# Constants behind the first graph's nodes, and the last two graphs' scaling re-divided between two engines

## The chip, the cores and the metric

The kernel runs on one core of a Trainium2 chip. The metric is the device time of one execution in microseconds (us), read as the median of several runs. A core has a matrix engine (TensorE, PE in the profile, with its weight loads listed apart as PEld), VectorE (DVE), ScalarE (ACT), GpSimd (POOL), and SyncE (SP), which in this kernel only issues transfers (DMA). Each engine works through its own queue of instructions in order, so an instruction that waits holds up all behind it on the same engine. Matrix products accumulate in PSUM, a small memory that TensorE writes and VectorE and ScalarE read; all other tiles lie in SBUF.

## The reference

Sixteen graphs (B = 16) of 1024 nodes with 256 features each pass two layers. `adj` is an integer matrix that holds only 0 and 1 here and is symmetric, so that of the four edge kinds of layer 0 only the one with weight vector `a0` occurs.

```python
# layer 0: gated aggregation
e0    = leaky(einsum('bid,bjd->bij', h * a0[:, 0], h))      # slope 0.2
alpha = sigmoid(where(adj == 1, e0, -max))                  # kinds 2 to 4 likewise with a1 to a3
x     = layernorm(x + einsum('bij,bjd->bid', alpha, h) + bias)

# layer 1: graph attention, 4 heads of 64 features
Wh    = (x @ W).reshape(B, N, 4, 64)
e     = leaky_relu(e_src[:, :, None] + e_dst[:, None, :])   # e_src = Wh.a_src, e_dst = Wh.a_dst per head
alpha = softmax(where(adj > 0, e, -1e9), axis=2)
x     = layernorm(x + elu(einsum('bijh,bjhf->bihf', alpha, Wh)))
```

## The kernel before

**Tiling.** Nodes go in 8 row blocks of 128 (index `jb` or `ib`), or in 2 halves of 512 columns, each half being two pairs of blocks. One graph is worked through in steps, and each step is a generator in `stages`; `issue` takes every step of every graph and issues them in the order of one number, `b * 112 + time`, where the times stand in three tables written into the kernel: `FIRST` for graph 0, `LAST` for graph 15 and `TIMES` for all others. Nothing reorders them afterwards, so these tables fix the order on every engine's queue. Steps of two to three neighbouring graphs are interleaved.

**Constants.** `load_constants` (L37 to L84) runs ahead of all graphs. On SP's queue it places the four columns `a_sb` (a0 to a3), the bias row, `w_aug` (the matrix W), then `a_src` broadcast to all partitions and `a_dst` in the same way. The two broadcast rows share one buffer, so `a_dst` (L63) waits until VectorE has multiplied W by `a_src`. VectorE forms the eight columns W·a_src and W·a_dst (four products of 128x256 and four sums), and the bias is split into a rounded high part and a rest (L75 to L83).

**Layer 0 of a graph.** `xload` (L237) brings the nodes `xb` (1 MB), `aload` (L243) brings one 512 KB block of the adjacency matrix at a time into one of two buffers `a32`, and `cast` (L252, ScalarE) turns it into bf16 in the single buffer `a16` and adds up its entries. `turn` transposes the block: graph 0 does so on TensorE, the other graphs by a DMA transpose. `mask` (L274, ScalarE) squares the transposed block into 8 bits, `mT`. Meanwhile the nodes are transposed (`xt`, `xtc`), scaled by a0 (`xta`), and multiplied (`score`); ScalarE and VectorE apply the leaky slope (`leak`, `leaky`), ScalarE the sigmoid. The scores are symmetric, so only the upper part is computed, and `lower` and `upper` (L379) multiply the mirrored and the direct part by the mask. `agg` (L390) aggregates over all blocks, and needs all eight masks. `residual`, `moments`, `spread` (GpSimd), `shift` and `norm` (L447, ScalarE) do the layer norm.

**Layer 1 of a graph.** `project` multiplies by `w_aug`, whose last eight columns give e_src and e_dst. `keep_rows` writes the e_src of each half as rows to DRAM (`sdram`), and `sload` reads the row of one head back, broadcast to 128 partitions (`sbc`). `exps` (L560 to L563) forms the exponentials `es` for both slopes s = 0 and 1, and `rho`. The exponential of a leaky sum is a product of a source and a target factor for each of the two slopes; so the kernel multiplies Wh by `es` (`product`, L576 on ScalarE for the last graph and L581 on VectorE for others), splits the result `gm` into a rounded high part (`high`, L594, ScalarE) and the rest (`low`, L601, VectorE), and multiplies by a matrix of zeros and ones, `pos` (L619, VectorE), that says at which edges the positive slope holds (`acc`, L631). The `gm` tile exists once, so the factors of the next graph come after the last product of this one that reads them. `acc` takes both PSUM buffers of its pool for one head in one half, and the next head begins when `acc_low` (L646, ScalarE) and `acc_sum` (L654, VectorE) have read both. `total` (L674) sums over all edges, which gives the negative slope by subtraction. `weigh` scales by `rho`, and `divide` takes the reciprocal `rzs` (L741) of the sum of the weights and scales by it; both scale through one helper, `times`: eight ScalarE instructions of one column factor each (L713) for the last graph, one VectorE instruction (L718) for the others. `elu`, `join`, and the second layer norm follow, and `leave` (L767) stores one half of 512 rows at a time.

**The end.** After the last graph, VectorE and TensorE reduce three checks (adjacency only 0 and 1, exponents in range, no overflow) to one `flag` (L1290), which the engines read; were it set, a slower general version would run. It is not set here.

Of the kernel before, what the change touches and what calls it, by code (L numbers as in the profile page):

```python
# [27 lines left out]
P = 128  # L28
HALF = 512
# [7 lines left out]
def load_constants(nc, const, work, x, a_list, bias, w, a_src, a_dst):  # L37
# [6 lines left out]
    k.F1 = F + 2  # L44
    k.ident = const.tile([P, P], F32, name="ident")
# [5 lines left out]

    k.a_sb = const.tile([P, k.DC, NK], F32, name="a_sb")
    for i, a in enumerate(a_list):
        nc.sync.dma_start(out=k.a_sb[:, :, i : i + 1], in_=a.rearrange("(c p) o -> p c o", p=P))
    bias_bc = work.tile([P, D], F32, tag="bias_bc", name="bias_bc")
    nc.sync.dma_start(out=bias_bc, in_=bias.partition_broadcast(P))


    k.w_aug = const.tile([P, k.DC, k.WD], F32, name="w_aug")
    nc.sync.dma_start(out=k.w_aug[:, :, 0:D], in_=w.rearrange("(c p) f -> p c f", p=P))  # L60
    for a, which in ((a_src, 0), (a_dst, 1)):
        a_bc = work.tile([P, D], F32, tag="a_bc", name=f"a_bc{which}")
        nc.sync.dma_start(out=a_bc, in_=a.rearrange("h f -> (h f)").partition_broadcast(P))  # L63
        for c in range(k.DC):
            prod = work.tile([P, D], F32, tag="prod", name=f"prod{which}_{c}")
            nc.vector.tensor_tensor(prod, k.w_aug[:, c, 0:D], a_bc, ALU.mult)
            dst = k.w_aug[:, c, D + which * H : D + which * H + H]
            nc.vector.tensor_reduce(dst, prod.rearrange("p (h f) -> p h f", h=H), AX.X, ALU.add)

# [5 lines left out]
    b_hi = work.tile([P, D], F32R, tag="b_hi", name="b_hi")  # L75
    nc.scalar.copy(b_hi, bias_bc)
    b_lo = work.tile([P, D], F32, tag="b_lo", name="b_lo")
    nc.vector.tensor_tensor(b_lo, bias_bc, b_hi.bitcast(F32), ALU.subtract)
    nc.vector.tensor_scalar(b_lo, b_lo, k.ident[:, 1:2], None, ALU.mult)
    k.bias_r = const.tile([P, D], F32R, name="bias_r")  # L80
    nc.vector.scalar_tensor_tensor(
        k.bias_r, b_hi.bitcast(F32), k.ident[:, 0:1], b_lo, ALU.mult, ALU.add
    )  # L83
    return k  # L84
# [105 lines left out]
class FastPools:  # L190
    def __init__(self, ctx, tc):
        def pool(name, bufs, **kw):
            return ctx.enter_context(tc.tile_pool(name=name, bufs=bufs, **kw))


        self.us = pool("f_us", 4)
        self.io = pool("f_io", 2)
        self.adjp = pool("f_adj", 2)
# [13 lines left out]
def stages(nc, k, pl, b, xg, adjg, outg, gm, sums, span, zinv):  # L212
# [9 lines left out]
    first, last = b == 0, b == k.B - 1  # L222
# [11 lines left out]

    def xload():
        t["xb"] = pl.io.tile([P, NB, D], F32, tag="xb", name="xb")
        nc.sync.dma_start(out=t["xb"], in_=xg.rearrange("(c p) d -> p c d", p=P))  # L237
        yield
# [186 lines left out]
    def spread(which):  # L425

        for half in range(NH):
            mvh = t["mv" + which][:, half * NQ : (half + 1) * NQ]
            v = small("std" + which, NQ)
            nc.gpsimd.tensor_scalar(v, mvh[:, :, 1], EPS, None, ALU.add)  # L430
            rstd = t["rstd" + which, half] = small("rstd" + which, NQ)
            nc.gpsimd.tensor_tensor(rstd, v, k.mhalf.to_broadcast([P, NQ]), ALU.pow)  # L432
            yield
# [9 lines left out]
    def norm(which):  # L443
        for ib in range(NB):
            half, q = divmod(ib, NQ)
            y = t["y", half][:, q, :]
            nc.scalar.activation(  # L447
                y, y, AF.Identity,
                bias=t["shift" + which, half][:, q : q + 1],
                scale=t["rstd" + which, half][:, q : q + 1],  # L450
            )
# [117 lines left out]
    def product():  # L569
        for h, s in FACTORS:  # L570
# [3 lines left out]
            if last:  # L574
# [16 lines left out]
    def high():  # L591
        for h, s in FACTORS:
            for cols, val in factor(h, s):
                nc.scalar.copy(gm[:, h, :, 0, s, cols], val)  # L594
# [746 lines left out]
```

## Time and profile before

| | us |
|---|---|
| runs, lowest to highest | 1781.34 to 1782.41 |
| runs, median of 3 | 1781.9 |
| the profiled execution's own time | 1781.79 |
| its span (first to last instruction) | 1780.0 |
| TensorE busy | 1718.5 |
| VectorE busy | 1624.8 |
| ScalarE busy | 1208.9 |
| GpSimd busy | 112.1 |

The page also cuts the span into 40 slices of 44.5 us and gives each engine's busy share in tenths:

```
PE   6999999999999999999999999999999999999883
DVE  4488999999999899999999999999999999999897
ACT  6583957759576684947759485784957668485665
PEclk9999999999999999999999999999999999999987
```

How to read it: a number after "L" is the line of the kernel; "out<-in" names the tiles that an instruction writes and reads; "xN" counts instructions; in square brackets stands the idle time of the engine ahead of the row, and the instruction whose end released it, as the profiler infers it. In a view in order of time, neighbouring instructions of one kind are put into one row with the start of the first. SPq is the queue of transfers that SP issues; a row there is the time of the issue, not of the transfer. The granted clock is the share of TensorE's full clock that the chip allowed.

### The profile page before, as it was taken

What the parts mean: (1) busy time and instruction counts of PE and PEld (TensorE: products, weight loads), DVE (VectorE), ACT (ScalarE), POOL (GpSimd) and SP (SyncE); (2) the same over time, 40 slices, a digit from 0 to 9 for tenths busy, and PEclk for the clock granted to TensorE, in tenths of its full rate; (3) what the DMA queues carried; (4) which work ended last, traced back from release to release, by engine and by line L of the source; (5) the groups of instructions that cost most, each with busy time, mean ns of one, the idle gap of its engine ahead of it and who ended that gap; (6) DMA issues with size and microseconds to landing.
All of it is one profiled execution on the core that took longest, in us unless ns stands there. A gap on an engine that the chain in (4) does not pass through costs nothing.

```text
span 1780.0 us, 29755 instructions
## 1 busy us (share of the span) xinstructions
PE 1718.5 (97%) x10707; PEld 1517.1 (85%) x10707; DVE 1624.8 (91%) x3581; ACT 1208.9 (68%) x2781; POOL 112.1 (6%) x138
## 2 busy tenths in 40 slices
PE   6999999999999999999999999999999999999883
PEld 4789898998979989898998979889898998989773
DVE  4488999999999899999999999999999999999897
ACT  6583957759576684947759485784957668485665
POOL 0000001010000101000010000101000010000100
PEclk9999999999999999999999999999999999999987
DMA  4452324524334343333424333353433425221020
GB/s 157 110 140 60 88 86 100 138 66 109 102 85 116 90 120 94 97 84 101 131 66 125 104 80 102 89 138 77 102 89 90 131 72 148 84 61 42 25 66 26
DMA packets 249243, 168.62 MB, mean 95 GB/s; under 512 B 133248, under 2 KB 232704, under 8 KB 249088
## 3 DMA queue, kind: packets, MB, share of 16 engines
q1 hardware_dynamic: 249088, 166.63, 35.0%
q8 instruction: 87, 1.43, 0.3%
q14 instruction: 68, 0.56, 0.1%
HBM read 118.10 MB, written 17.04 MB: 76 GB/s over the span
## 4 chain that ended last, share of the span: by engine, by line
PE 86%; issue 8%; ACT 2%; DVE 1%; POOL 1%; DMA 0%; POOLq 0%; ACTq 0%
PE acc L631 25%; PE agg L390 23%; PE tot L674 13%; PE e L323 13%; PE pw L479 6%; PE pg L362 3%; PE pt L287 1%; PE pt L460 1%; PE agg L386 1%; POOL rstd L432 1%; DVE pos L619 0%; ACT gm L594 0%; ACT a L252 0%; PE pbc L553 0%; ACT L349 0%
## 5 line engine op out<-in xcount | busy, mean ns | idle before, releaser
L619 DVE SCALAR_TENSOR_TENSOR pos<-sbc,nd,mT 128x512 fp32r<-128x512 f32 x1024 | 730.9, 743 | 35.6 <-PE acc L631 34.9
L631 PE MATMUL acc<-gm,pos 128*128 128x264 f32 x4096 | 629.0, 299 | 17.9 <-DVE rzs L741 6.0
L631 PEld LDWEIGHTS acc<-gm,pos 128*128 128x128 f32 x4096 | 547.7, 191 | 41.5 <-issue 15.9
L390 PE MATMUL agg<-xb,gate 128*128 128x256 f32 x2048 | 473.6, 379 | 0.0
L390 PEld LDWEIGHTS agg<-xb,gate 128*128 128x128 f32 x2048 | 374.0, 190 | 44.0 <-DVE gate L379 0.2
L674 PE MATMUL tot<-gm,allm 128*128 128x264 f32 x2048 | 321.3, 298 | 0.0
L674 PEld LDWEIGHTS tot<-gm,allm 128*128 128x128 f32 x2048 | 280.4, 189 | 4.0
L646 ACT COPY low<-acc 128x264 f32<-128x264 f32 x256 | 90.3, 378 | 279.9 <-PE acc L631 279.7
L323 PE MATMUL e<-xT,xTa 128*128 128x512 f32 (+3 forms) x768 | 269.2, 487 | 3.3 <-ACT xTa L311 1.6
L323 PEld LDWEIGHTS e<-xT,xTa 128*128 128x128 f32 x768 | 131.5, 190 | 92.8 <-issue 45.6
L666 ACT CAST allm<-mT 128x512 fp32r<-128x512 uint8 x256 | 157.0, 619 | 35.3 <-PE tot L674 34.9
L447 ACT ACTIVATE y<-y,shift,rstd 128x256 f32<-128x256 f32 x256 | 137.8, 592 | 45.1 <-DVE shift L440 45.0
L252 ACT ACTIVATE a<-a 128x1024 bf16<-128x1024 int32 x128 | 135.6, 1059 | 15.4 <-DMA aT<-a 7.9
L274 ACT ACTIVATE mT<-aT 128x1024 uint8<-128x1024 bf16 x120 | 127.1, 1059 | 16.0 <-DMA aT<-a 15.9
L430 POOL TENSOR_SCALAR std<-mv 128x4 f32<-128x4 f32 x64 | 30.1, 470 | 1653.1 <-DVE mv L413 1565.9
L479 PE MATMUL pw<-w_aug,yT 128*128 128x264 f32 x512 | 124.5, 386 | 0.5 <-ACT yT L469 0.5
L654 DVE TENSOR_TENSOR u<-acc,low 128x264 f32<-128x264 f32 x256 | 104.6, 420 | 12.8 <-ACT low L646 12.6
L343 DVE TENSOR_TENSOR gate<-e,gate 128x512 f32<-128x512 f32 x192 | 104.3, 551 | 9.2 <-ACT gate L335 8.8
L335 ACT ACTIVATE gate<-e 128x512 f32<-128x512 f32 x192 | 93.6, 488 | 18.4 <-PE e L323 18.3
L479 PEld LDWEIGHTS pw<-w_aug,yT 128*128 128x128 f32 x512 | 92.5, 190 | 13.8 <-ACT yT L469 1.3
L407 DVE BATCH_NORM_STATS2 st<-y 128x6 f32<-128x256 f32 x256 | 102.4, 415 | 0.6
L379 DVE TENSOR_TENSOR gate<-gate,mT 128x1024 f32<-128x1024 f32 (+7 forms) x128 | 95.0, 751 | 0.9 <-ACT mT L274 0.6
(101 smaller groups left out, 1817.2 us busy)
## 6 DMA issues: line engine op xcount, KB each, us to landing
a<-in_adj_dram SPq DMA_DIRECT2D x128, 512.0 KB, 4.9
sbc<-sdram SPq DMA_DIRECT2D x128, 256.0 KB, 4.5
xb<-in_x_dram SPq DMA_DIRECT2D x16, 1024.0 KB, 5.7
out_dram<-y SPq DMA_DIRECT2D x32, 512.0 KB, 3.5
aT<-a SPq DMA_TRANSPOSE x120, 3.1
sdram<-srow SPq DMA_DIRECT2D x32, 8.0 KB, 1.4
w_aug<-in_L_gnn_W_dram SPq DMA_DIRECT2D x1, 256.0 KB, 4.5
bias_bc<-in_L_gnn_bias_dram SPq DMA_DIRECT2D x1, 128.0 KB, 3.8
```

The costliest lines, as they stand in the source:

```text
L252: nc.scalar.activation(t["a16", ib], t["a32", ib], AF.Copy, accum_out=sums[:, 0, at : at + 1])
L274: nc.scalar.activation(t["mT"][:, :, ib * P : (ib + 1) * P], t["aT", ib], AF.Square, accum_out=sums[:, 1, at : at + 1],)
L323: nc.tensor.matmul(e[:, 0:n], lhsT=t["xTa", jb][:, c, :], rhs=t["xT"][:, c, at : at + n], start=(c == 0), stop=(c == DC - 1),)
L343: nc.vector.tensor_tensor(ge, t["e", jb, at][:, 0:n], ge, ALU.max)
L390: nc.tensor.matmul(agg[:, 0:D], lhsT=t["gate"][:, jb, ib * P : (ib + 1) * P], rhs=t["xb"][:, jb, :], start=False, stop=(jb == NB - 1),)
L447: nc.scalar.activation(y, y, AF.Identity, bias=t["shift" + which, half][:, q : q + 1], scale=t["rstd" + which, half][:, q : q + 1],)
L479: nc.tensor.matmul(pw[:, 0:WD], lhsT=t["yT"][:, c, jb * P : (jb + 1) * P], rhs=k.w_aug[:, c, :], start=(c == 0), stop=(c == DC - 1),)
L619: nc.vector.scalar_tensor_tensor(p_, t["sbc", half, h], t["nd"][:, jb, h : h + 1], t["mT"][:, jb, half * HALF : (half + 1) * HALF], ALU.is ...
L631: nc.tensor.matmul(t["acc", half, h, q // 2][:, q % 2, 0 : 4 * F1], lhsT=t["pos", half, h, jb][:, q * P : (q + 1) * P], rhs=gm[:, h, jb].r ...
L654: nc.vector.tensor_tensor(t["u", half, pair][:, :, h, :], t["acc", half, h, pair][:, :, 0 : 2 * F1], t["low", half, h, pair], ALU.add,)
L666: nc.scalar.copy(m_, t["mT"][:, j0 : j0 + 4, ib * P : (ib + 1) * P])
L674: nc.tensor.matmul(tot[:, 0 : H * F1], lhsT=t["allm", ib, jb // 4 * 4][:, jb % 4, :], rhs=gm[:, :, jb, l, 1, :], start=(jb == 0 and l == 0 ...
```

## The change

The change has five parts.

1. *Loading.* `load_constants` is divided into `shapes`, `make_constants` and a step `setup` of the first graph. `FastPools` opens the pools of nodes and adjacency first and the others later, in `fill`. Ahead of everything, graph 0's nodes are requested, in two halves, and its first two adjacency blocks; then `make_constants` requests only the column of `a0`. The five parts of `setup`, which do something in graph 0 only, are: request the two broadcast rows (each now with its own space) and W; form the eight weight columns; request the bias row and the other three columns; round the bias; form its rest. Their tiles come from the tag `sbc`, four buffers, which the products and the broadcast rows use later.
2. *Scaling.* In `times`, the ScalarE form holds for the last two graphs (14 and 15), where it held for the last one.
3. *Products.* In the last graph, ScalarE forms only the products of slope s = 1; those of s = 0 go to VectorE.
4. *Norm and store.* In the last graph's second half, the second norm of every other block goes to VectorE as one instruction of two scalars. The last half is stored in two parts.
5. *Order.* `FIRST` and `LAST` hold new times for all steps. `TIMES` is unchanged but for a row for `setup`, which does nothing there. `gm` is reached as `pl.gm`, and `rstd` is allocated ahead of `std`; neither alters an instruction.

```diff
-def load_constants(nc, const, work, x, a_list, bias, w, a_src, a_dst):
+def shapes(x, a_src):
     k = Consts()
...
+    return k
+
+def make_constants(nc, k, const, work):
...
-    for i, a in enumerate(a_list):
-        nc.sync.dma_start(out=k.a_sb[:, :, i : i + 1], in_=a.rearrange("(c p) o -> p c o", p=P))
-    bias_bc = work.tile([P, D], F32, tag="bias_bc", name="bias_bc")
-    nc.sync.dma_start(out=bias_bc, in_=bias.partition_broadcast(P))
...
+    a0 = k.inputs[0][0]
+    nc.sync.dma_start(out=k.a_sb[:, :, 0:1], in_=a0.rearrange("(c p) o -> p c o", p=P))
...
 class FastPools:
     def __init__(self, ctx, tc):
...
+        self.io = self.pool("f_io", 2)
+        self.adjp = self.pool("f_adj", 2)
+
+    def fill(self):
...
-    first, last = b == 0, b == k.B - 1
+    first, last, late = b == 0, b == k.B - 1, b >= k.B - 2
...
+    def two(name, dtype=F32):
+        tile = pl.work.tile([P, 2, D], dtype, tag="sbc", name=name, bufs=4)
+        return tile[:, 0], tile[:, 1]
+
+    def setup():
+        if not first:
+            yield from (None for _ in range(5))
+            return
+        a_list, bias, w, a_src, a_dst = k.inputs
+        rows = two("vecs")
+        for row, a in zip(rows, (a_src, a_dst)):
+            nc.sync.dma_start(out=row, in_=a.rearrange("h f -> (h f)").partition_broadcast(P))
+        nc.sync.dma_start(out=k.w_aug[:, :, 0:D], in_=w.rearrange("(c p) f -> p c f", p=P))
+        yield
+
+        for which in range(2):
+            for c, prod in enumerate(two("wa")):
+                nc.vector.tensor_tensor(prod, k.w_aug[:, c, 0:D], rows[which], ALU.mult)
+                dst = k.w_aug[:, c, D + which * H : D + which * H + H]
+                nc.vector.tensor_reduce(
+                    dst, prod.rearrange("p (h f) -> p h f", h=H), AX.X, ALU.add
+                )
+        yield
+
+        row, low = two("brow")
+        nc.sync.dma_start(out=row, in_=bias.partition_broadcast(P))
+        for i in range(1, NK):
+            nc.sync.dma_start(
+                out=k.a_sb[:, :, i : i + 1], in_=a_list[i].rearrange("(c p) o -> p c o", p=P)
+            )
+        yield
+        high, _ = two("bhigh", F32R)
+        nc.scalar.copy(high, row)
+        yield
+        nc.vector.tensor_tensor(low, row, high.bitcast(F32), ALU.subtract)
+        nc.vector.tensor_scalar(low, low, k.ident[:, 1:2], None, ALU.mult)
+        nc.vector.scalar_tensor_tensor(
+            k.bias_r, high.bitcast(F32), k.ident[:, 0:1], low, ALU.mult, ALU.add
+        )
+        yield
+
     def xload():
         t["xb"] = pl.io.tile([P, NB, D], F32, tag="xb", name="xb")
-        nc.sync.dma_start(out=t["xb"], in_=xg.rearrange("(c p) d -> p c d", p=P))
+        parts = NH if first else 1
+        for i in range(parts):
+            c = slice(i * NB // parts, (i + 1) * NB // parts)
+            nc.sync.dma_start(
+                out=t["xb"][:, c, :], in_=xg.rearrange("(c p) d -> p c d", p=P)[:, c, :]
+            )
         yield
...
+            if last and which == "1" and half and q % 2:
+                nc.vector.tensor_scalar(y, y, rstd, shift, ALU.mult, ALU.add)
+            else:
+                nc.scalar.activation(y, y, AF.Identity, bias=shift, scale=rstd)
...
-            if last:
+            if last and s:
                 for jb in range(NB):
                     nc.scalar.activation(
                         prod[:, jb, :], t["wh"][:, jb, h * F : (h + 1) * F], AF.Copy,
...
     def times(val, by):
-        if last:
+        if late:
...
         for half in range(NH):
-            nc.sync.dma_start(
-                out=outg[half * HALF : (half + 1) * HALF].rearrange("(c p) d -> p c d", p=P),
-                in_=t["y", half],
-            )
+            parts = 2 if last and half else 1
+            rows = outg[half * HALF : (half + 1) * HALF].rearrange("(c p) d -> p c d", p=P)
+            for i in range(parts):
+                c = slice(i * NQ // parts, (i + 1) * NQ // parts)
+                nc.sync.dma_start(out=rows[:, c, :], in_=t["y", half][:, c, :])
...
 FIRST = {
-    "xload": [-2609.24],
-    "aload": [-1820.92, -1748.01, -1728.96, -1693.97, -1643.68, -1598.12, -1550.35, -1517.97],
+    "aload": [-144.60, -143.90, -143.00, -141.40, -140.70, -140.00],
+    "cast": [-144.70, -144.30, -143.50, -142.40, -141.10, -140.60, -139.50, -138.20],
+    "setup": [-143.30, -141.90, -141.00, -139.70, -138.80],
...
 LAST = {
-    "product": [93.84, 98.53, 107.41, 108.99, 117.90, 120.96, 121.69, 130.00],
-    "high": [101.62, 105.85, 109.82, 112.50, 120.77, 125.89, 130.29, 131.74],
+    "product": [87.30, 106.33, 109.41, 112.35, 128.05, 129.38, 131.00, 134.97],
+    "high": [87.97, 112.70, 115.38, 121.19, 130.65, 133.04, 133.80, 135.49],
-    "sload": [97.90, 120.51, 140.05, 147.06, 613.52, 2137.72, 2152.35, 2712.83],
+    "sload": [94.08, 134.36, 137.42, 163.52, 2179.14, 3774.53, 4722.65, 4722.85],
...
+        k = shapes(x, a_src)
+        k.inputs = (a0, a1, a2, a3), bias, w, a_src, a_dst
+        pl = FastPools(fast, tc)
...
+        for name in ("xload", "aload", "aload"):
+            next(graphs[0][name])
         with tc.tile_pool(name="first", bufs=1) as first:
-            k = load_constants(nc, const, first, x, (a0, a1, a2, a3), bias, w, a_src, a_dst)
...
+            make_constants(nc, k, const, first)
+        pl.fill()
```

## The prediction

> **What bounds the kernel now.** I read the page first, then busy time by stage, then the start and the end in order of time, and last the waits of SP's queue and the groups that the change touches. First the page's engine row, then six stretches of the span (columns: stretch, length, busy time of PE, PEld, DVE, ACT and POOL, granted TensorE clock, DMA share, GB/s).
>
> ```profile
> PE 1718.5 (97%) x10707; PEld 1517.1 (85%) x10707; DVE 1624.8 (91%) x3581; ACT 1208.9 (68%) x2781; POOL 112.1 (6%) x138
> ```
>
> ```profile
> 0.00:40.00 40.00, 23.34 (x127) 14.68 (x128) 15.93 (x42) 25.70 (x47) 1.27 (x10) 1.00 0.54 175
> 226.00:1600.00 1374.00, 1373.04 (x8575) 1214.42 (x8574) 1306.06 (x2871) 951.33 (x2153) 90.87 (x104) 1.00 0.38 100
> 1656.00:1690.00 34.00, 28.06 (x173) 25.55 (x172) 30.01 (x79) 23.61 (x72) 2.94 (x4) 0.96 0.04 10
> 1690.00:1712.00 22.00, 13.51 (x77) 13.06 (x77) 20.46 (x47) 17.23 (x59) 0.00 (x0) 0.67 0.20 60
> 1712.00:1740.00 28.00, 28.00 (x227) 28.00 (x226) 26.77 (x52) 16.62 (x44) 2.03 (x2) 1.00 0.19 57
> 1760.00:1780.00 20.00, 0.37 (x1) 0.08 (x1) 9.49 (x33) 11.25 (x35) 2.53 (x4) 0.50 0.18 57
> ```
>
> From 226 to 1600 TensorE misses 1 us of 1374: nothing that leaves its work alone can gain there. It is idle for 16.7 us before 40, for 14.4 between 1656 and 1712, and nearly always after 1760. The change must win at the two ends. The start in order of time (start, duration, engine, line, what):
>
> ```profile
> 4.26 0.43 SPq L237 DMA_DIRECT2D xb<-in_x_dram  x1
> 4.74 0.58 SPq L243 DMA_DIRECT2D a<-in_adj_dram  x1
> 9.98 0.34 SPq L63 DMA_DIRECT2D a_bc<-in_L_gnn_a_dst_dram  x1
> 13.06 1.06 ACT L252 ACTIVATE a<-a 128x1024 bf16<-128x1024 int32 x1 [5.89 <-DMA a<-in_adj_dram]
> 38.29 1.06 ACT L274 ACTIVATE mT<-pa 128x1024 uint8<-128x1024 bf16 x1
> 39.47 1.23 DVE L379 TENSOR_TENSOR gate<-gate,mT 128x1024 f32<-128x1024 f32 x1 [0.19 <-ACT mT L274]
> ```
>
> The nodes are requested at 4.26, behind seven constant loads; then SP's queue stands until 9.98, because the second broadcast row needs the buffer of the first, so the second adjacency block goes out at 10.36. The last mask (38.29) releases the first masked gate row (39.47), and that the aggregation, from where TensorE is full until 82. So the start is a chain: first block landed, eight casts and eight masks on ScalarE, aggregation. The end, TensorE alone, then three VectorE and ScalarE rows of the closing:
>
> ```profile
> 1688.26 6.79 PE L631 MATMUL acc<-gm,pos 128*128 128x264 f32 x32 [5.15 <-DVE gm L601]
> 1701.08 0.78 PE L631 MATMUL acc<-gm,pos 128*128 128x264 f32 x2 [6.02 <-DVE rzs L741]
> 1704.32 3.42 PE L631 MATMUL acc<-gm,pos 128*128 128x264 f32 x14 [2.47 <-ACT gm L594]
> ```
>
> ```profile
> 1703.75 0.43 DVE L654 TENSOR_TENSOR u<-acc,low 128x264 f32<-128x264 f32 x1
> 1771.29 2.07 ACT L447 ACTIVATE y<-y,shift,rstd 128x256 f32<-128x256 f32 x4 [0.50 <-DVE shift L440]
> 1772.73 0.14 DVE L1290 TENSOR_SCALAR flag<-good 1x1 int32<-1x1 f32 x1
> ```
>
> The releasers named at 1701.08 and 1704.32 only stand beside the true ones: head 1 needs both PSUM banks of head 0 emptied, and VectorE's two sums stand at 1700.51 and 1703.75, queued behind the low halves of gm, which wait for ScalarE's products and casts (gm done at 1704.7).
>
> **The change part by part.** Instruction order: from the 864th to the 8109th TensorE matmul (the middle of graph 1 to graph 14) both kernels issue the same. All sums are against the profiled execution: span 1780.0, its time 1781.8; the median of the runs is 1781.9, so a gain carries over unchanged.
>
> *First loads.* Removed ahead of the nodes: the four a_sb, bias, w, a_src (seven issues of 0.43 to 0.5 us). SP's order becomes nodes in two halves, adjacency 0 and 1, one a_sb, adjacency 2 and 3, the two rows and w, adjacency 4 and 5, bias and three a_sb, adjacency 6 and 7. Adjacency 0 goes out at 0.73+2x0.48 = 1.7 instead of 4.74. Before, it landed 8.3 us after issue (13.04), with 2.0 MB sent since 2.76, part of it slow broadcast rows (115 GB/s in 4 to 6 us, 358 and 368 in 8 to 12). Now 1.5 MB of plain rows lie ahead of its end: from about 2.0 (DMA begins after the first issue at 0.73) at 363 GB/s that is 4.2 us, landed at 6.3; with the old 8.3 us, at 10.0. I take 7.0, near the lower end, because the slow broadcasts are gone: the first cast is 6.0 us earlier (3.0 to 6.7). A rule speaks against splitting: the Trainium skill, "DMA: Bandwidth & Descriptors", section Bandwidth, wants transfers of 1 MiB or more, and Anatomy of one DMA gives each about 2.0 us plus bytes at 436 GB/s. One 512 KB block alone takes 3.1 to 3.3 us here, which fits. Were transfers served one by one, three would be over at 0.7+9.6 = 10.3 and the gain 2.7. But in 8 to 12 us, with the 1 MB and the 0.5 MB transfer in flight, the row is 358 to 368 GB/s: overlapped, they pay it once. I side with the row.
>
> *From first cast to last mask.* Before: 13.06 to 39.35, 26.3 us, of which ScalarE idles about 3, 1.6 of it for the second block. After, by the new order, with cast and mask 1.05 and 1.0, leak 0.45, table and sigmoid 2.25: cast 0 at 7.0; scores of row 0 wait for a_sb (fifth on the queue, about 8.7) and for VectorE, and stand before turn 0 on TensorE, so turn 0 ends at 10.6 and cast 1, which needs its buffer, starts there; cast 2 at 14.1, cast 3 at 16.5, cast 4 at 20.3, cast 7 at 29.9, last mask over at 32.6. That is 6.7 earlier, from which I take 0.4, since one sigmoid (0.98 us) that used to precede the last mask now follows it. Blocks 2 to 7 still leave when a cast frees one of two buffers and land 3.3 us later, within the 3.7 us between casts; the rows and w (0.5 MB, 1.4 us) delay block 4 by no more than the slack after cast 2. Eight weight products on VectorE (0.42 each, 3.4 in all) and three bias steps (1.2) fall where it is busy 16 of 40 us; behind them wait xTa of row 2 on. ScalarE's bias cast (0.4) waits for a row requested nine us earlier. Without that cover, the 3.4 would be added once. **Start: -6.3** (-2.5 to -7.5). The aggregation (32 us of full TensorE) and all behind it only shift; ScalarE's bound stretch 80 to 112 (31.8 of 32 busy) loses one cast of 0.6 to an earlier place.
>
> *Graph 14's scales on ScalarE* (two rho and two reciprocal groups in each half). The groups:
>
> ```profile
> L718 DVE TENSOR_TENSOR u<-u,rho 128x528 f32<-128x528 f32 x60 | 41.4, 690 | 0.0
> L713 ACT ACTIVATE u<-u,rho 128x66 f32<-128x66 f32 x32 | 8.2, 338 | 2.1 <-DVE u L701 1.1 <-DVE u L725 1.0
> L79 DVE TENSOR_SCALAR b_lo<-b_lo,ident 128x256 f32<-128x256 f32 x1 | 0.3, 344 | 0.0
> ```
>
> VectorE sheds 8x0.62 = 5.0 us; ScalarE gains 8 groups of eight, 2.0 us each (eight take 2.03 at 1738.29), 15.8 in all. In the first half TensorE is full and ScalarE idle half the time: 0, unless an eviction queued behind a group holds TensorE up (at most 2 us each).
>
> *Products of the last graph.* The four s=0 products go to VectorE (4x0.60 = 2.4 us) and leave ScalarE (4x2.0 = 8.0). Walking the new order from the exponentials es (L560), which start at 1680.4: ScalarE's gm ends at 1680.4+24.3-8.0+2.0 (one rho group now ahead)+1.2 (a third norm and a low ahead) = 1699.9 instead of 1704.7. VectorE's last low half is over at 1700.9, then two pos, one add and the second sum of head 0: 1703.3 instead of 1704.1. But TensorE has twelve totals placed before head 1, which run at 1700.9 instead of idling. A rule enters: the Trainium skill, "TensorE: Matmul & The Clock Gate", Part 1, says an idle window of about 3.4 us halves the clock and as much busy time restores it. The row 1690 to 1712 shows 0.67, and 32 acc took 6.79 us there against 0.13 each in 1712 to 1740. The new order keeps a hole of 6 us before 1700.9, so the twelve cost 2.6 us, not 1.5, and still end about when the sum does: 2.4 us of lead by the rule, 2.7 at the warm rate; I take the first. VectorE's queue confirms it: twenty pos and graph 14's zinv are done at 1713.3 instead of 1715.8. In the last head five pos, not six, follow the sum that frees its banks: 0.5 more. The second sdram half leaves late, at about 1708, for a row read first after 1720. **Tail: -2.9** (-5 to +1, the upper end if two evictions slip by 2 us each).
>
> *Norm shared and last store in two.* Two ScalarE steps take 1.08 instead of 2.07, while VectorE does two of 0.34: -1.0 at the last store, perhaps 0.3 more for its smaller half. But the flag (1772.73) now stands 0.7 later, and the span ends 7 us after it and 3 us after the store's landing; which of them holds it no row tells. Between +0.7 and -1.3; I take **-0.6**.
>
> Sum: -6.3-2.9-0.6 = -9.8: span 1770.2, median **1772.1**.
>
> **The rivals.** *Start alone* (the tail's two holes stay: ScalarE trades 8.0 us of products for 8.0 of graph 14's second half, and VectorE 2.4 for 2.5; the closing hangs on the flag): -6.3, 1775.6. For it: the trade is even; against: the weigh groups stand behind most of gm. *Serial loads* (a_sb or the block is late): -2.7-3.5, 1775.7. *Nothing arrives* (both of these): 1779 to 1780. *Slower*: the groups of ScalarE, placed before PSUM evictions in graph 14. All eight exposed cost 15.8 us; with -7.3 from start and closing that is 1790.4, and slower by 0.2% needs 10.9 of the 15.8, seven tenths, on TensorE's path. Against: ScalarE is 28 of 56 us busy in 1600 to 1656.
>
> **How the numbers follow.** 0.2% (3.6 us) is about what a measurement of this kernel tells from no change. Both ends gain 0.60, start alone 0.15, serial loads 0.13, nothing 0.08, slower 0.04. Faster 0.88, same 0.08, slower 0.04. The range ends low where start and tail reach their better bounds together, less what is improbable (-14), and high at the edge of "nothing": 1768.0 to 1778.5.
>
> **What would show it.** First cast near 7 and the last mask near 32.6 (right), or beyond 36 (serial). The aggregation starts near 34. Stretch 226 to 1600, shifted, still full. The last graph's last gm cast ends 19.5 us after es starts (before: 24.3); head 1 resumes 23 us after es. The last norm takes 1.1 us, and the span's end after it stays at 6.6 or grows by up to 1. Wrong it is if gaps appear in TensorE in the 80 us before es of the last graph, or if the hole before the aggregation closes no earlier although the cast does.

## The result, and the profile after

The changed kernel takes 1773.7 us (median of 6 runs, 1772.2 to 1775.0) against 1781.64 us before (6 runs, 1780.8 to 1783.2). The ratio is 0.9954, with a 95% interval from 0.9942 to 0.9967: 7.9 us faster, between 6 and 10. The profiled execution took 1773.8 with a span of 1772.0 (before: 1780.0), so the two traces differ by 8.0, and the sums below are made against that.

The engine row of the page of the changed kernel shows the same work as before, in 8 us less:

```profile
PE 1719.8 (97%) x10707; PEld 1516.2 (86%) x10707; DVE 1622.6 (92%) x3579; ACT 1211.6 (68%) x2809; POOL 111.1 (6%) x138
```

Busy time by stage of the changed kernel (stretch, length, busy time of PE, PEld, DVE, ACT and POOL, granted clock, DMA share, GB/s). The first is the same 40 us as shown of before; the others lie 6 to 8 us earlier than their counterparts.

```profile
0.00:40.00 40.00, 29.68 (x148) 18.04 (x149) 18.88 (x47) 28.33 (x53) 1.26 (x10) 1.00 0.56 175
220.00:1594.00 1374.00, 1374.00 (x8590) 1216.09 (x8589) 1306.99 (x2874) 952.91 (x2157) 91.57 (x104) 1.00 0.38 99
1648.00:1682.00 34.00, 30.83 (x195) 28.01 (x193) 28.72 (x77) 21.94 (x66) 4.49 (x6) 1.00 0.11 32
1682.00:1704.00 22.00, 13.90 (x72) 13.35 (x73) 20.99 (x45) 21.64 (x79) 0.00 (x0) 0.69 0.15 48
1704.00:1732.00 28.00, 26.98 (x216) 26.72 (x216) 27.27 (x57) 14.94 (x37) 1.26 (x2) 1.00 0.24 67
1752.00:1772.00 20.00, 0.37 (x1) 0.08 (x1) 10.56 (x36) 10.39 (x33) 3.32 (x4) 0.50 0.17 57
```

The middle is as full as before (1374.00 of 1374). TensorE has done 6.3 us more within the first 40. The hole ahead of head 1 (fourth row) is still there, but ScalarE, which stood at 17.2 of 22 there, is now full (21.6) beside VectorE (21.0).

The start of the changed kernel in order of time (start, duration, engine, line, what, and in brackets the idle time before it):

```profile
1.78 0.97 SPq L275 DMA_DIRECT2D a<-in_adj_dram  x2
2.80 0.43 SPq L65 DMA_DIRECT2D a_sb<-in_L_gnn_a_dram  x1
7.90 1.06 ACT L284 ACTIVATE a<-a 128x1024 bf16<-128x1024 int32 x1 [5.88 <-DMA a<-in_adj_dram]
9.44 0.87 DVE L341 TENSOR_SCALAR xTa<-xT,a_sb 128x128 f32<-128x128 f32 x4 [0.67 <-DMA a_sb<-in_L_gnn_a_dram]
9.87 3.54 PE L355 MATMUL e<-xT,xTa 128*128 128x512 f32 x4 [0.98 <-DVE xTa L341]
13.94 1.06 ACT L284 ACTIVATE a<-a 128x1024 bf16<-128x1024 int32 x1 [4.71 <-PE pa L294]
35.27 1.02 ACT L306 ACTIVATE mT<-pa 128x1024 uint8<-128x1024 bf16 x1 [0.23 <-PE pa L294]
36.41 1.22 DVE L411 TENSOR_TENSOR gate<-gate,mT 128x1024 f32<-128x1024 f32 x1 [0.65 <-ACT mT L306]
37.89 1.89 PE L422 MATMUL agg<-xb,gate 128*128 128x256 f32 x8
```

The first block is cast at 7.90, 5.2 earlier than before. The second is cast at 13.94, only 1.9 earlier: ScalarE waits 4.71 for the transposes of the first block. These stand on TensorE behind the first four scores, which waited for the column of a0 (asked for at 2.80, landed at 9.34, 6.5 later) and then took 3.54 us where before they took 1.96. The same places before:

```profile
15.83 1.06 ACT L252 ACTIVATE a<-a 128x1024 bf16<-128x1024 int32 x1 [1.61 <-PE pa L262]
16.53 1.96 PE L323 MATMUL e<-xT,xTa 128*128 128x512 f32 x4 [0.79 <-DVE xTa L309]
```

From the second cast to the aggregation it takes 24.0, before 24.9. So the aggregation starts 2.9 earlier, not 6.3.

The end on TensorE, then two rows of the closing. The exponentials of the last graph start at 1677.28 (before 1680.44):

```profile
1685.00 5.97 PE L664 MATMUL acc<-gm,pos 128*128 128x264 f32 x32 [6.16 <-DVE gm L634]
1696.67 2.79 PE L707 MATMUL tot<-gm,allm 128*128 128x264 f32 x11 [0.51 <-DVE gm L634]
1699.25 1.08 PE L664 MATMUL acc<-gm,pos 128*128 128x264 f32 x4
...
1738.31 3.92 PE L664 MATMUL acc<-gm,pos 128*128 128x264 f32 x30 [0.43 <-DVE u L687]
1744.17 4.54 PE L664 MATMUL acc<-gm,pos 128*128 128x264 f32 x32 [1.94 <-DVE u L687]
...
1763.40 1.09 ACT L484 ACTIVATE y<-y,shift,rstd 128x256 f32<-128x256 f32 x2 [2.04 <-DVE shift L472]
1765.62 0.14 DVE L1325 TENSOR_SCALAR flag<-good 1x1 int32<-1x1 f32 x1
```

Head 1 resumes at 1699.25, 22.0 after the exponentials (before 1704.32, 23.9 after), behind the twelve totals. For the last two heads, these are the rows of before. TensorE stood idle for 3.22 ahead of the first of them, and both took longer:

```profile
1745.13 5.76 PE L631 MATMUL acc<-gm,pos 128*128 128x264 f32 x32 [3.22 <-DVE u L654]
1751.58 5.07 PE L631 MATMUL acc<-gm,pos 128*128 128x264 f32 x32 [0.70 <-DVE u L654]
```

Marks read from both traces in this way give a ledger of the 8.0 us:

| stretch | before | after | gain | forecast |
|---|---|---|---|---|
| to the start of graph 0's aggregation | 40.75 | 37.89 | 2.9 | 6.3 |
| to the exponentials of graph 15 | 1639.69 | 1639.39 | 0.3 | 0 |
| to head 1 resuming | 23.88 | 21.97 | 1.9 | 0.9 |
| to graph 14's `zinv` on VectorE | 11.42 | 10.90 | 0.5 | 1.5 |
| to the end of the last `acc` | 40.91 | 38.56 | 2.4 | 0.5 |
| to the last `shift` | 14.44 | 14.50 | -0.1 | 0 |
| to the end of the span | 8.91 | 8.79 | 0.1 | 0.6 |
| sum | 1780.0 | 1772.0 | 8.0 | 9.8 |

Each column is one execution, and other profiled executions of the same instructions show how firm two of the gains are. With the whole new tail, head 1 resumes 22.0 to 22.2 after the exponentials in eight kernels. With the old tail it is 23.9, 23.6 and 22.6 in three; the 32 products ahead of the hole took 6.79, 6.50 and 5.52 there, and what follows them is equal to 0.02. So the 1.9 can be as little as 0.7. The 2.4 of the last heads is 1.2 in three of the ten kernels with the new tail. Both go with the granted clock (last section).

### The profile page after: what moved, and what is told of

It reads as the page before. It is cut to its first block, busy times and chain, and to the rows that moved or that the text cites. A ratio compares the mean times of both kernels' runs of the same rounds, so it can differ in the third digit from the quotient of the medians.

```text
span 1772.0 us, 29785 instructions
## 1 busy us (share of the span) xinstructions
PE 1719.8 (97%) x10707; PEld 1516.2 (86%) x10707; DVE 1622.6 (92%) x3579; ACT 1211.6 (68%) x2809; POOL 111.1 (6%) x138
## 4 chain that ended last, share of the span: by engine, by line
PE 92%; issue 5%; ACT 1%; DMA 1%; DVE 1%; POOL 0%; SPq 0%; POOLq 0%; ACTq 0%; DVEq 0%
PE acc L664 26%; PE agg L422 25%; PE tot L707 14%; PE e L355 13%; PE pw L512 6%; PE pg L394 3%; PE pt L493 2%; PE pt L319 1%; PE agg L418 1%; ACT a L284 0%; DMA a_sb<-in_L_gnn_a_dram 0%; ACT mT L306 0%; DMA a<-in_adj_dram 0%; PE pbc L586 0%; POOL rstd L464 0%
## 5 line engine op out<-in xcount | busy, mean ns | idle before, releaser
L652 DVE SCALAR_TENSOR_TENSOR pos<-sbc,nd,mT 128x512 fp32r<-128x512 f32 x1024 | 728.8, 740 | 37.8 <-PE acc L664 36.6
L664 PE MATMUL acc<-gm,pos 128*128 128x264 f32 x4096 | 626.2, 298 | 10.3 <-DVE gm L634 6.2
L699 ACT CAST allm<-mT 128x512 fp32r<-128x512 uint8 x256 | 156.9, 619 | 24.9 <-PE tot L707 24.4
L284 ACT ACTIVATE a<-a 128x1024 bf16<-128x1024 int32 x128 | 135.6, 1059 | 19.5 <-DMA a<-in_adj_dram 8.1
```

The lines of the kernel that those rows point to most:

```text
L284: nc.scalar.activation(t["a16", ib], t["a32", ib], AF.Copy, accum_out=sums[:, 0, at : at + 1])
L652: nc.vector.scalar_tensor_tensor(p_, t["sbc", half, h], t["nd"][:, jb, h : h + 1], t["mT"][:, jb, half * HALF : (half + 1) * HALF], ALU.is ...
L664: nc.tensor.matmul(t["acc", half, h, q // 2][:, q % 2, 0 : 4 * F1], lhsT=t["pos", half, h, jb][:, q * P : (q + 1) * P], rhs=pl.gm[:, h, jb ...
L699: nc.scalar.copy(m_, t["mT"][:, j0 : j0 + 4, ib * P : (ib + 1) * P])
```

## The experiments

A ratio stands with its 95% interval, which is 1.3 to 2.5 us to each side, so effects of 1 us are read from the marks of the one profiled execution of each kernel. The two theories at the outset: the prediction's (the start brings 6.3 and the tail 3.5), and that of the ledger (the start, held by the scores and a0's column, brings 3, the tail 5).

**Start and tail apart.** First the changed kernel with the old tail: the table `LAST` of before with a row for `setup` (which does nothing there), the last norm on ScalarE alone, the last store whole, and

```diff
-        if late:
+        if last:
...
-            if last and s:
+            if last:
```

> The changed kernel with the whole tail of before: LAST as before, graph 14 scaled on VectorE, all eight products of the last graph on ScalarE, norm and store whole. The prediction's ledger (start -6.3) gives 1775.5 against 1781.6 before; the ledger read from the two traces (aggregation of graph 0 at 37.9 instead of 40.75, exponentials of the last graph 3.2 earlier) gives -2.9 to -3.2, so 1778.5. A rival in which the gain of the start is eaten before the tail gives 1781.

Measured: 1777.1 against 1782.0, ratio 0.9971 (0.9959 to 0.9983). The median is 4.9 less, with an interval of 3.0 to 7.3 that holds both theories' 6.1 and 3.1. The profiled execution was the longest of the six (1775.8 to 1778.7), with a span of 1776.9, 3.1 less. In it the aggregation starts at 38.18 and the exponentials of graph 15 are 3.3 earlier than before; from there to the end it takes 99.7, as before (99.6). By these marks the second theory holds. The six times fall in two groups of three, 2 us apart in the mean, which would fit the two durations of the first scores (below), but only one was profiled. Then the kernel before with the new tail: the new `LAST` without its row for `setup`, norm and store as in the changed kernel, and the two edits reversed:

```diff
-        if last:
+        if late:
...
-            if last:
+            if last and s:
```

> The kernel before with the last graph's table, scaling, products, norm and store of the changed kernel, and its own start. The prediction's ledger (-2.9 and -0.6) gives 1778.1; the ledger read from the traces (from the exponentials of the last graph to the end 4.8 less) gives 1776.8. If start and tail only gain together, about 1781.

Measured: 1778.0 against 1782.0, ratio 0.9978 (0.9970 to 0.9985), 4.0 less; this median is nearer to the prediction's 1778.1 than to 1776.8. The profiled execution was the shortest of the sixteen, with a span of 1775.5; from the exponentials to the end it takes 95.1 instead of 99.6, 4.5 less, nearer to the second theory. The two spans add to 7.6 of the 8.0, the medians to 8.9 of 7.9, which their intervals allow. So the ends gain independently; how the gain is divided between them is told by the traces alone.

**The first transposes ahead of the first scores.**

```diff
     "score": [
-        -144.80, -144.20, -143.80, ...
+        -144.35, -144.20, -143.80, ...
```

> The changed kernel with one number of FIRST altered: the first scores stand behind the first adjacency transposes on TensorE instead of ahead of them. If the column of a0, which lands at 9.3, is what holds up the cast of the second block (13.9), by way of the scores that wait for it, that cast comes at 9.7 to 10.5 and the last mask and the aggregation come 2 to 4 us earlier: 1770 to 1772. If ScalarE's chain is held by the transfers instead, the cast moves but the aggregation stays within 0.5 us: 1773.5.

Measured: 1771.8, ratio 0.9941 (0.9927 to 0.9954), the lowest median of all, though its interval overlaps that of the change. ScalarE and TensorE in order of time:

```profile
9.70 1.06 ACT L284 ACTIVATE a<-a 128x1024 bf16<-128x1024 int32 x1 [0.58 <-PE pa L294]
...
13.93 1.02 ACT L306 ACTIVATE mT<-pa 128x1024 uint8<-128x1024 bf16 x1 [1.57 <-PE pa L294]
...
35.22 1.89 PE L422 MATMUL agg<-xb,gate 128*128 128x256 f32 x8
```

The second cast comes 4.2 earlier (9.70), as expected if the scores held it. The aggregation comes 2.7 earlier, but not all of that is the order, as the next group shows.

**What the scores of the first graph take.** Five profiled kernels have the start of the changed kernel unaltered. In four of them the first four scores took 3.54 to 3.75 us and the aggregation began at 37.6 to 38.2. In one, whose edit lies in the last graph (the products, below), they took 1.95:

```profile
9.78 1.95 PE L355 MATMUL e<-xT,xTa 128*128 128x512 f32 x4 [0.83 <-DVE xTa L341]
...
12.27 1.06 ACT L284 ACTIVATE a<-a 128x1024 bf16<-128x1024 int32 x1 [3.16 <-PE pa L294]
...
36.07 1.89 PE L422 MATMUL agg<-xb,gate 128*128 128x256 f32 x8
```

So the same program takes 1.6 to 1.8 us longer over these scores or not, and the aggregation follows. In the kernel with the first transposes ahead they took 1.96; against the short form of the unaltered start (36.07), its order is worth 0.9. With other orders of the split start (below) they took 1.96 to 2.82.

Is it the clock? In the changed kernel the last three of the four start 0.85 us apart, in the short form 0.43. The scores of graph 1 are the same kind of product, and there the recorded clock does change. Two stretches of the changed kernel, the first with graph 0's scores, the second with graph 1's (granted clock third from the end):

```profile
9.87:13.20 3.33, 3.33 (x4) 1.30 (x5) 1.04 (x4) 0.00 (x0) 0.00 (x0) 1.00 0.51 157
85.00:88.00 3.00, 3.00 (x4) 1.14 (x4) 2.45 (x6) 3.00 (x8) 0.00 (x0) 0.50 0.51 191
```

In the second stretch, too, the scores start 0.85 apart, and behind it, at 1.00, 0.43. So the first scores run as at half the clock, though the record has 1.00 there in every kernel: that it is the clock is argued from the durations and not shown.

Graph 1's scores have a lesson of their own, which the ledger hides in its middle. In all ten kernels with the new start TensorE is idle for 1.98 ahead of them. The changed kernel, the one with the products on ScalarE, and the one with norm and store undone:

```profile
83.81 10.12 PE L355 MATMUL e<-xT,xTa 128*128 128x512 f32 x20 [1.98 <-ACT xTa L343]
81.99 11.39 PE L355 MATMUL e<-xT,xTa 128*128 128x512 f32 x20 [1.98 <-ACT xTa L343]
83.53 8.55 PE L355 MATMUL e<-xT,xTa 128*128 128x512 f32 x20 [1.98 <-ACT xTa L343]
```

The same twenty scores take about 8.55 in five of the ten (granted clock 1.00 from 80 to 90), 10.12 in four and 11.39 in one (below 1.00 for a part of it). In that one, the lead of 1.8 that the short scores of graph 0 gave is gone when the exponentials of graph 15 begin (1677.49; 1677.28 in the changed kernel). A lead at the start is not yet a lead at the end.

In the next run the nodes came in one piece:

```diff
-        parts = NH if first else 1
+        parts = 1
```

> The changed kernel with the first graph's nodes in one transfer of 1 MB instead of two of 512 KB. If queued transfers overlap and pay their fixed time once, the split costs one issue (0.5): the first cast comes at 7.4 instead of 7.9, the first node transposes at 6 instead of 4.7, and the aggregation stays within 0.7 of 37.9. If each transfer paid its fixed 2 us in turn, the first cast would come at 5.9.

Measured: 1773.7, ratio 0.9957 (0.9943 to 0.9970), as with the split. The first cast comes at 7.63, within the 7.52 to 7.90 of the five executions with the split: the issue that was expected to go (0.5) does not show. It is far from the 5.9 of transfers that pay in turn, so they overlap. The sixteen transposes run in one go from 6.46, the scores are short, and the aggregation comes 1.3 earlier, more than the 0.7 expected:

```profile
10.32 1.96 PE L355 MATMUL e<-xT,xTa 128*128 128x512 f32 x4 [0.42 <-DVE xTa L341]
...
36.56 1.89 PE L422 MATMUL agg<-xb,gate 128*128 128x256 f32 x8
```

The split lets the transposes begin 1.8 earlier (4.71), but puts gaps of 0.27 and 0.98 ahead of the scores. In four profiled kernels with the start of before, nodes whole, the scores took 1.95 to 2.41. That the split makes the long form likelier fits these ten kernels, but it is not shown: there is one execution of this kernel, and the gap alone does not decide, for the scores were short behind a gap of 0.83 (products on ScalarE) and long behind 0.61 (norm and store undone). Nodes in one piece together with the first transposes ahead was not tried.

**The column of a0 first**, moved out of `make_constants`:

```diff
+        k.a_sb = const.tile([P, k.DC, NK], F32, name="a_sb")
+        nc.sync.dma_start(out=k.a_sb[:, :, 0:1], in_=a0.rearrange("(c p) o -> p c o", p=P))
         for name in ("xload", "aload", "aload"):
             next(graphs[0][name])
```

> The changed kernel with the column of a0 requested ahead of the nodes instead of fifth. If its landing (6.5 us after its issue, behind 2 MB) is due to its place, it lands near 3, the first adjacency block 0.5 later than 7.9, and the first scores start when the transposed nodes are there, near 9.2: aggregation 0.3 to 1 us earlier, 1773. If tiny pieces are slow wherever they stand and delay the others, the nodes land 1 to 2 us later and the kernel ends 1 to 2 us later, 1775.

Measured: 1773.2, ratio 0.9954 (0.9940 to 0.9967). VectorE no longer waits for the column, and the first block is cast at 8.54 (0.6 later). But the scores start at 10.31, 0.4 later than in the changed kernel and not near 9.2, since the nodes are later too: their last twelve transposes begin at 7.27 instead of 6.07. The second cast comes at 13.44 and the aggregation at 37.19. That is 0.7 earlier, in the expected range by luck: the scores took 2.60 instead of 3.54, and this 0.9 is more than the whole gain. The column's landing was one wait of two that end together, the other being the transposed nodes.

**Both transposes early**: the edit of the first transposes and this one, without and with the column first:

```diff
-    "turn": [-144.40, -144.10, ...
+    "turn": [-144.40, -144.25, ...
```

> The kernel with the first transposes ahead of the first scores, and the second transposes ahead of the second scores as well. There ScalarE waits 1.6 us (12.4 to 13.9) for the second transposed block behind those scores; if that wait is on the path, the aggregation comes 1 to 1.5 us earlier than 35.2, and the kernel ends at 1770 to 1771; if not, 1771.8.

> Both transposes early, and the column of a0 requested ahead of the nodes. With the casts no longer behind the scores the column's landing should matter little: as with the transposes alone or up to 0.7 us better or worse (the first block lands 0.6 later), 1770 to 1771.5.

Measured: 1772.0 (0.9946, 0.9933 to 0.9960) and 1773.1 (0.9949, 0.9935 to 0.9962); aggregation at 35.74 and 36.54. No further gain, against expectation: the mask that waited 1.57 now starts at 12.64, but ScalarE waits again, 0.65 at 15.9, for the scores that were put back. In the first of the two, four scores from 23.18 on also take 3.04 at a granted clock of 0.50 for a part, where the order with the first transposes ahead took 1.94; so the two orders are not told apart by their aggregations. From 10 to 34 ScalarE is busy 22.2 of 24 us in both, so little is left there. With the column first the four first scores took 2.82.

**Graph 14's scaling back on VectorE.**

```diff
-        if late:
+        if last:
```

> The changed kernel, but graph 14 scaled on VectorE again, in the same places of the order. VectorE, full in the hole ahead of head 1 (21.0 of 22 us busy), gets four groups more there (2.5 us), ScalarE loses 8: if VectorE sets the end of the hole, head 1 resumes 1 to 2.5 us later (22.0 after the exponentials now) and the kernel ends that much later, 1775 to 1776. If ScalarE sets it, it gets faster, 1771 to 1773.

Measured: 1773.8, ratio 0.9957 (0.9943 to 0.9970); span 1773.5. The medians don't tell (the profiled execution was the longest of the five). The trace does: head 1 resumes 23.2 after the exponentials (22.0 to 22.2 in the eight kernels with the whole new tail), `zinv` follows 10.9 after that as with the change, and the rest is equal. So this part is worth 1.0 to 1.2, within what was expected if VectorE sets the end of the hole.

**The products back on ScalarE**, in the new order:

```diff
-            if last and s:
+            if last:
```

> The changed kernel, but all eight products of the last graph on ScalarE again, in the same order. ScalarE, 21.6 of 22 us busy in the hole, gets 8.0 us more, VectorE loses 2.4: head 1 resumes 3 to 6 us later and the kernel ends at 1777 to 1780 if the products on ScalarE hold the hole open; within 1 us of 1773.5 if VectorE does.

Measured: 1780.1, ratio 0.9991 (0.9983 to 0.9999). TensorE at the hole:

```profile
1703.03 0.59 PE L707 MATMUL tot<-gm,allm 128*128 128x264 f32 x1 [8.71 <-ACT gm L627]
1703.95 2.79 PE L707 MATMUL tot<-gm,allm 128*128 128x264 f32 x11 [0.33 <-DVE gm L634]
1706.54 1.08 PE L664 MATMUL acc<-gm,pos 128*128 128x264 f32 x4
```

Head 1 resumes 29.0 after the exponentials (1677.49), 7.1 later than with the change, more than the 3 to 6 expected: nearly all of ScalarE's 8 us is on the path. **The products alone**, in the old order of before:

```diff
-            if last:
+            if last and s:
```

> The kernel before with one part of the change alone: the four products of slope 0 of the last graph on VectorE, everything else and the whole order as before. If ScalarE's products hold the hole ahead of head 1 open whatever the order, its 8.0 us less there close the hole by 2 to 5 us (head 1 resumes 19 to 22 after the exponentials, 23.9 before): 1777 to 1780. If the gain needs the new order too, since the low halves and the sums stand behind other work on VectorE, head 1 resumes within 1 us of before: 1781 to 1782.

Measured: 1782.3 against 1781.95, ratio 1.0005 (0.9997 to 1.0013): nothing. VectorE's second sum and TensorE:

```profile
1704.41 0.43 DVE L654 TENSOR_TENSOR u<-acc,low 128x264 f32<-128x264 f32 x1
...
1704.99 3.42 PE L631 MATMUL acc<-gm,pos 128*128 128x264 f32 x14 [2.22 <-DVE u L654]
```

ScalarE finishes its casts 22.3 after the exponentials (1680.81) instead of 24.3, and stands idle for 3.9 us in between, but the sum that frees the banks stands 23.6 after the exponentials (before 23.3): VectorE has four products more in its queue and works without a pause from 1694.8 up to this sum. Head 1 resumes at 24.2. Shared products gain nothing in the old order, and the new order without them is 7 behind the new order with them: the two are one step.

**The last heads' sums.** In the kernel before, four numbers of the last graph's table:

```diff
     "acc_low":  ...
-        2904.38, 3107.19, 3108.34, 3297.28, ...
+        2904.38, 3043.50, 3043.52, 3297.28, ...
     "acc_sum":  ...
-        2909.06, 3108.21, 3127.76, 3316.46, ...
+        2909.06, 3043.55, 3043.57, 3316.46, ...
```

> The kernel before with four numbers of LAST altered: in the last graph, the two sums that empty the PSUM buffers for head 2 of the second half stand on VectorE ahead of a join, a subtraction, one pos and the second join instead of behind them (2.2 us of VectorE work). If these sums set the hole of 3.2 us in TensorE at 1741.9 and the slower clock behind it (32 products in 5.8 us instead of 4.5), the hole shrinks to about 1 and the end comes 2 to 2.5 us earlier: 1779.5 against 1781.9. If VectorE's own work is the bound there, the hole moves to the next head and the end comes 0 to 0.5 earlier.

Measured: 1780.7 against 1781.3, ratio 0.9995 (0.9987 to 1.0003). TensorE's last two heads:

```profile
1743.17 2.78 PE L631 MATMUL acc<-gm,pos 128*128 128x264 f32 x20 [1.01 <-DVE u L654]
1747.45 2.15 PE L631 MATMUL acc<-gm,pos 128*128 128x264 f32 x12 [1.50 <-DVE pos L619]
1750.58 5.06 PE L631 MATMUL acc<-gm,pos 128*128 128x264 f32 x32 [0.99 <-DVE u L654]
```

The hole of 3.2 is down to 1.0 as expected, but 1.5 of it comes back inside the head, where a `pos` is late: the two joins still stand ahead of it. From `zinv` to the last `acc` it takes 39.8 instead of 40.9, against 38.6 in the changed kernel: a half of that gain, between the two expectations. The other half is VectorE's whole queue. Busy time from `zinv` to the last `acc`, before:

```profile
1715.74:1740.00 24.26, 24.26 (x198) 24.26 (x197) 23.04 (x44) 13.95 (x38) 0.00 (x0) 1.00 0.22 66
1740.00:1756.70 16.70, 12.73 (x80) 11.47 (x78) 14.78 (x29) 7.37 (x26) 0.00 (x0) 0.90 0.01 1
```

And in the changed kernel:

```profile
1710.15:1734.40 24.25, 23.23 (x187) 22.97 (x187) 23.82 (x45) 13.56 (x38) 0.00 (x0) 1.00 0.23 66
1734.40:1748.72 14.32, 11.19 (x84) 10.24 (x82) 13.73 (x28) 6.25 (x23) 0.00 (x0) 1.00 0.01 2
```

VectorE does 37.8 us of work in 41.0 before and 37.6 in 38.6 after: it is the bound of this stretch, and the new order takes 2.1 of its 3.1 us of waiting away.

**Norm and store undone.**

```diff
-            if last and which == "1" and half and q % 2:
-                nc.vector.tensor_scalar(y, y, rstd, shift, ALU.mult, ALU.add)
-            else:
-                nc.scalar.activation(y, y, AF.Identity, bias=shift, scale=rstd)
+            nc.scalar.activation(y, y, AF.Identity, bias=shift, scale=rstd)
-            parts = 2 if last and half else 1
+            parts = 1
```

> The changed kernel with the last norm on ScalarE alone and the last store in one piece. The prediction has -0.6 for the two, so 1774.3; by the traces the span ends 8.8 us after the last shift with them and 8.9 without, so no change: 1773.7.

Measured: 1772.0, ratio 0.9950 (0.9936 to 0.9963): not slower than with both parts (0.9942 to 0.9967). From the last `shift` to the end 8.9, with both parts 8.8.

## Why the prediction was right, and where it missed

The forecast of 1772.1 (1768.0 to 1778.5) holds the 1773.7, and its likeliest case, that both ends gain and the middle only shifts, is what start and tail alone show. But the total is closer than its terms, and that is luck: the start brought 3.4 less, the closing 0.5 less, the tail 1.8 more and the middle 0.3. TensorE is busy 79.4 of the 80 us ahead of the last exponentials (79.2 before), so that sign of an error is absent. Its matmuls still differ in order up to the 1009th, not only to the 863rd; nothing hung on it.

*First loads: right.* The first block was put at 7.0 where the row of overlapped transfers was preferred to one transfer after the other (10.3). It is cast at 7.90, 0.9 later than that and 2.4 earlier than the other. The whole transfer of the nodes (7.63) agrees: a further transfer in the queue costs no more than its issue. The fit that the prediction cites is given on that page for transfers that GpSimd issues, and here SP issues them, so the measured 3.1 to 3.3 us is the ground. The rival of serial loads had the start at 2.7, nearer to the 2.9, but little of it by its own cause: the block was not late, and the column by 0.6.

*From first cast to last mask: the step that failed*, in its words "scores of row 0 wait for a_sb ..., so turn 0 ends at 10.6 and cast 1 ... starts there". It starts at 13.94. Of the 3.3 us, 0.6 is the column (9.34 instead of 8.7; it stood behind 2 MB in its queue and took 6.5 us, where before, at the front, such columns took 2.1). The Trainium skill, "DMA: Bandwidth & Descriptors", section Queues, rings and completion order, says that each DMA engine takes descriptors in ring order, and this agrees. About 1.1 was an error of the sum: from 8.7, the scaling (0.3), four scores (1.96 in the row of before) and the transposes (0.45) lead to 11.4, not to 10.6, and in the kernel with the short scores the cast comes 3.0 after the column. And 1.6 is the long form of the scores, which the prediction did not consider, though it counted on a halved clock in the hole of the tail. With short scores the start gains 4.7 to the aggregation (36.07). From the second cast to the last mask it forecast 22.0, and 22.4 were measured.

*Setup work on VectorE: right.* The eight products stand at 20.8 to 24.0, and TensorE's next wait (1.73, to 24.96) is for a cast of ScalarE, not for them.

*The tail: mechanism right, sizes off.* ScalarE's last `gm` was forecast 19.5 after the exponentials and came 18.4 after (1695.63), because the 24.3 of before held a wait of 1.15 for head 0 that the sum carried along. Head 1 was forecast at 23.0 and came at 22.0. "Start alone", the rival in which the trade is even, falls: the products alone in the old order gain nothing, as it says, but with the order they are worth 7. The rival that ScalarE's groups block evictions falls too: they are worth a gain of 1.0 to 1.2. (Its start and closing are 6.9 by the terms, not the 7.3 that it subtracts.) `zinv` was forecast at 32.9 after the exponentials and stands at 32.9, by luck: head 1 is 1.0 earlier than forecast, and from it to `zinv` it takes 1.0 more. The halved clock on which the sum counted there came: the eleven totals took 2.79, 0.25 each, at a granted 0.53 from 1695.6 to 1699.2. What the prediction sized at 0.5, the last heads, measured 2.4 (1.2 where the last head ran at the lower clock): it looked at one sum and its five `pos`, not at the hole of 3.2 ahead of the last head but one, or at VectorE's waits there.

*Norm and store: wrong, too small to matter.* 0.1, not 0.6. ScalarE's norm is 1.0 shorter, and the end comes 7.5 after it instead of 6.6. The sum knew that no row shows whether the flag or the store holds the end, and this stays open: with both parts undone the end lies as far behind the last shift (8.9 and 8.8).

## What to carry to other kernels

When a transfer is moved to the front, follow the next instruction of each engine's queue: here the block came 5 us earlier, and its transposes stood on TensorE behind scores that needed another transfer. Work shared between two engines pays only if the order on both queues lets it; cost the pair, and subtract the waits of the old order before re-using its distances. Before a difference of 1 or 2 us between two traces is put down to an order, see whether the products behind each gap of TensorE ran at the same pace in both. A stretch whose bound is VectorE is read from VectorE's idle time in it, not from TensorE's holes, which move when one of them is closed.

## What the runs showed of the hardware

A gap of TensorE that is the same to 0.04 us can cost 1.3 us or nothing. Before the last head, ten profiled kernels with the new tail have the same 32 products and a gap of 1.92 to 1.96 us ahead of them. In seven the 32 products take 4.54, in three 5.84 to 5.86. Busy time and granted clock (third number from the end) of the kernel with norm and store undone, whose last head starts at 1742.47:

```profile
1742.40:1743.90 1.50, 1.43 (x10) 1.31 (x11) 1.50 (x6) 0.26 (x2) 0.00 (x0) 0.99 0.00 0
1743.90:1745.40 1.50, 1.50 (x9) 1.50 (x9) 1.50 (x3) 1.50 (x8) 0.00 (x0) 0.50 0.00 0
1745.40:1746.90 1.50, 1.50 (x9) 1.50 (x9) 1.03 (x4) 0.26 (x2) 0.00 (x0) 0.50 0.00 0
```

And of the changed kernel, whose last head starts at 1744.17:

```profile
1744.20:1745.70 1.50, 1.50 (x11) 1.38 (x12) 1.50 (x4) 0.36 (x2) 0.00 (x0) 1.00 0.00 0
1745.70:1747.20 1.50, 1.50 (x15) 1.50 (x14) 1.50 (x4) 1.50 (x7) 0.00 (x0) 1.00 0.00 0
```

In the first the clock falls to a half 1.4 us after work has resumed and stays there for about 3 us; in the second it stays full. Behind the gap of 1.98 near 82 the same happens to graph 1's scores (8.55, 10.12 or 11.39), there in five of ten, and in the kernel before the clock is 0.50 from 1688 to 1694, under 32 products that took 6.79. The Trainium skill, "TensorE: Matmul & The Clock Gate", Part 1, describes free-running windows of about 3.4 us, so that it matters where a gap falls in them. This fits what differs between equal kernels, but no trace here shows the windows; and the page's table has the clock fall after an idle window, where here a gap of 1.9 us, well short of one, is enough. For this case it means that a gain of 1 us ahead of such a gap can be taken back or doubled by the clock behind it: the nodes in one piece had the exponentials 1.2 earlier than the changed kernel and ended only 0.7 earlier, with a last head of 5.84.
